# Two PSUM banks in turn for the scan's sums, a later turned copy, and column sums with standing ones

## The chip, the cores and the metric

The kernel runs on one core of one Trainium2 chip. A core has a tensor engine (PE, whose weight loads are shown apart as PEld), a vector engine (DVE), a scalar engine (ACT), GpSimd (POOL) and a sync engine (SP) that issues the DMA transfers here. Each engine works through its own queue in order and waits on semaphores for the others. On-chip memory is SBUF, and PSUM, in eight banks of 2 KiB in each of 128 partitions, takes what PE writes. The metric is the device time of one execution in microseconds (us); 13 runs are shown, and the median counts.

## The reference

The input is four images of 64x64 positions with 96 channels. Layer 0 normalises by groups, multiplies by signs of a weight, runs a 3x3 convolution on signs, and then a selective scan in four directions (by rows, by columns and both reversed) with 192 channels and 16 states each. Its core is one recurrence:

```
def step(h, inp):
    ut, dt, Bt, Ct = inp
    dA = jnp.exp(dt[..., None] * A[None])
    h = dA * h + (dt * ut)[..., None] * Bt[:, :, None, :]
    y = jnp.einsum('bkdn,bkn->bkd', h, Ct)
    return (h, y)
```

`dt` (delta) is the softplus of a small matmul of signs plus a bias. The four directions are added, normalised over channels, gated, and projected. Layer 1 is a linear attention (keys times values first) and a feed-forward layer whose numbers are rounded to small floats.

## The kernel before, in words

**The scan.** `Scans.run` (L1323) goes through 1536 pieces, each a tile of 128 partitions by 1024 positions in float32. A piece has 32 channels with 4 states each, so four pieces (q = 0..3) make a group of channels, and eight pieces fill one tile of sums. One turn of the loop, step i, issues for the pieces around i:

- `loads` and `load_sums`: DMA transfers on SP, ahead of need;
- `carry(i-1)` (L1271): ACT copies the last column of the last scan, the state that the next chunk of the same rows starts from;
- at i % 8 == 3, `evacuate(i-4)` (L1316): ACT copies the finished tile of sums `yp` to SBUF as `ys`, and SP stores it;
- `decay(i+1)` (L1231): ACT makes exp(delta·A), the tile `dA`, in PSUM. Two tiles of 128x1024 (four banks in all) are shared by all pieces, and a pool gives out whichever came free;
- `reduce(i-3)` (L1302): PE adds the products of a piece over its four states into the tile `yp` (four matmuls, each into 32 partitions), and the other directions' sums (L1307);
- `inject(i+4)`: POOL multiplies delta·u by B, the tile `w`, four pieces ahead of its scan; nine such tiles exist;
- `late_product` and `scan(i)`: DVE runs the recurrence. Either it does so in place, in dA, and DVE multiplies by C; or it writes to a tile `h` in SBUF, and POOL multiplies by C one step later. A planner (`Tally`) that adds up an estimate of both engines' work picks one, piece by piece. All DVE and POOL operations of these kinds have the line of the planner's helper, L401, and are told apart by their tiles.

**Delta, in lanes.** `prepare` (L1130) makes delta for 512 positions of 128 rows. It is a generator, and each of its parts is issued in one step, so the parts of one lane lie between the scans: eight matmuls into a tile `dps` (L1167); ACT's Abs and Relu (L1172, L1173); ACT's Exp and Ln (L1175, L1176, the latter back into the bank of `dps`); a matmul by the identity that adds the Relu (L1179); DVE's product `pd` by u; and ACT's copy of delta (L1185) with the stores. A lane starts at each i % 8 == 0, 192 in all, of which three are made before the first scan.

**Work behind.** A second generator, `back`, issues a part at each step: the prologues of the coming images (the normalisation, the convolution), and the epilogues (layer norms, attention, feed-forward). Where a lane needs u that isn't there yet, `back` is run on until it is.

The convolution in the prologue (L567 to L633) goes part by part, 8 rows of 64 at a time. A part has four steps; PE issues 5, 4, 5 and 4 of the 18 taps (L577) in them, while ACT and DVE finish the part before: signs and exp at step 1, log and exp at step 2, DVE's product `u` at step 3, and in that step also the copy of u by columns `ut`, on POOL for the first image (when no scans run) and on ACT (L614) for the others. After four parts the turned tile is stored to `utd`, from which the prologue's next stage loads it; its cast is `xr` (L659).

The group normalisation starts with sums over positions (L508 to L517): 32 matmuls (L510) that hold a 128x96 tile of x as weights and move one column of ones, all added into 96x1, copied by ACT (L514) and multiplied by a matrix that adds three channels (L516).

**PSUM.** Four of the eight banks hold the two tiles `dA`. The other four are tags of a pool with one buffer each: `b0` and `b1` for prologue and epilogue, `y` for the sums and `dps` for delta.

Of the kernel before, what the change touches and what calls it, by code (L numbers as in the profile page):

```python
# [24 lines left out]
NT = L // 128  # L25
# [28 lines left out]
def hybrid_kernel(ctx: ExitStack, tc: tile.TileContext, a: dict, out: bass.AP):  # L54
# [102 lines left out]
    def weights():  # L157
# [28 lines left out]
        def transposed(dst, srcs):  # L186

            count[0] += 1
            ps = p.ps.tile([128, 1024], BF16, name=f"tps{count[0]}", tag=("y", "dps")[count[0] % 2])
            at = 0  # L190
            for src in srcs:
                n, f = src.shape
                nc.tensor.transpose(ps[:f, at : at + n], src, identb[:n, :n])
                at += n
            nc.vector.tensor_copy(dst, ps[:f, 0:at], saturate=False if dst.dtype == F8 else None)
# [152 lines left out]
        nc.vector.tensor_copy(  # L348
            back4.rearrange("p (x d) -> p x d", x=4), ident.rearrange("p (x d) -> p x d", x=4)[:, ::-1, :]
        )  # L350
        ps = p.ps.tile([128, 512], F32, name="tpd", tag="dps")
        for g in range(3):
            for x in range(4):
                nc.tensor.matmul(
# [122 lines left out]
def prologue(c, b, xts=None):  # L477
# [11 lines left out]
    with tc.tile_pool(name=f"xg_{b}", bufs=1) as xgp:  # L489
# [3 lines left out]
        with tc.tile_pool(name=f"cv_{b}", bufs=1) as cvp:  # L493
# [6 lines left out]
            if xts is None:  # L500
# [4 lines left out]
                load_x(c, b, xts)  # L505
                yield
                yield
            csum = bank("csum", 0)[0:96, 0:1]  # L508
            for i in range(NT):
                nc.tensor.matmul(csum, xts[i // 8][:, i % 8, :], c.ones1, start=(i == 0), stop=(i == NT - 1))  # L510
                if i % 8 == 7:
                    yield
            cs = f32("cs")[0:96, 0:1]
            nc.scalar.copy(cs, csum)  # L514
            gsum = bank("gsum", 1)[0:96, 0:1]
            nc.tensor.matmul(gsum, c.grp, cs, start=True, stop=True)  # L516
            yield  # L517
            negm = f32("negm")[0:96, 0:1]
# [42 lines left out]
            parts = [(h, q) for h in range(2) for q in range(NQ8)]  # L561
            taps = [(j, t) for j in range(2) for t in range(9)]
            one = lambda h: slice(h, h + 1)
            prev = None
            two = c.p.dA.tile([128, CH], F32, name=f"cv2_{b}", tag="dA") if alone else None
            utp = sub.enter_context(tc.tile_pool(name=f"ut_{b}", bufs=1))
            for n, part in enumerate(parts + [None]):  # L567
                if part:
                    h, q = part
                    nm = f"{h}{q}"  # L570
                    at = 512 * (n % 2)
                    ps = (two[:, at : at + 512] if alone else bank("cv" + nm, 0))[0:96]
                for s in range(4):
                    if part:
                        for j, t in taps[(0, 5, 9, 14)[s] : (5, 9, 14, 18)[s]]:
                            dy, dx = divmod(t, 3)
                            nc.tensor.matmul(  # L577
                                ps, c.cw[:, j, t, 96 * h : 96 * h + 96],
                                tpad[j][:, 8 * q + dy : 8 * q + dy + 8, dx : dx + IW],
                                start=(j == 0 and t == 0), stop=(j == 1 and t == 8),  # L580
                            )
                    if prev:
                        ph, pq, pz, v, r, pn = prev
                        if s == 0:
                            c.vec.scalar_tensor_tensor(pz, pz, pv[:, ph, S_X : S_X + 1], v, ALU.mult, ALU.add)
                            c.vec.scalar_tensor_tensor(pz, r, c.oma[:, one(ph)], pz, ALU.mult, ALU.add)
                        elif s == 1:

                            sg = f32("sg" + pn)[0:96, 0:128]
                            nc.scalar.activation(  # L590
                                sg.bitcast(F8).rearrange("p (h e i) -> p h e i", h=8, e=2),
                                pz.rearrange("p (h i e) -> p h e i", h=8, e=2), AF.Sign, saturate=False,
                            )
                            for m in range(3):
                                g0 = 64 * (m // 2) + 32 * ph
                                c.later.store(xgw[g0 : g0 + 32, m % 2, 128 * pq : 128 * pq + 128], sg[m::3, :])
                            e = f32("e" + pn)[0:96]
                            nc.scalar.activation(e, pz, AF.Exp, scale=-1.0)
                        elif s == 2:
                            nc.scalar.activation(e, e, AF.Ln, bias=1.0)  # L600
                            nc.scalar.activation(e, e, AF.Exp, scale=-1.0)
                        else:
                            u = f32("u" + pn)[0:96]
                            c.vec.tensor_tensor(u, pz, e, ALU.mult)
                            c.later.store(c.ud[b][ph][:, 512 * pq : 512 * pq + 512], u)

                            if pq % 4 == 0:
                                ut = utp.tile([96, IW, 32], F32, name=f"ut{pn}_{b}", tag="ut")
                            at = 8 * (pq % 4)
                            dst, src = ut[:, :, at : at + 8], u.rearrange("p (h w) -> p w h", w=IW)  # L610
                            if alone:
                                nc.gpsimd.tensor_copy(dst, src)
                            else:
                                nc.scalar.copy(dst, src)  # L614
                            if pq % 4 == 3:
                                rows = slice(8 * pq - 24, 8 * pq + 8)
                                c.later.store(
                                    c.utd[b][ph].rearrange("p (w h) -> p w h", h=IH)[:, :, rows], ut, after=1
                                )
                    yield  # L620
                if part:
                    v, r = f32("v" + nm)[0:96], f32("r" + nm)[0:96]
                    if alone:
                        nc.vector.tensor_scalar(v, ps, c.acs[:, one(h)], c.acb[:, one(h)], ALU.mult, ALU.add)
                    else:
                        nc.scalar.activation(v, ps, AF.Identity, scale=c.acs[:, one(h)], bias=c.acb[:, one(h)])
                    nc.scalar.activation(r, ps, AF.Relu, scale=c.csc[:, one(h)], bias=c.cbias[:, one(h)])  # L627
                    pz = bank("cz" + nm, n % 2 if alone else 1)[0:96]
                    nc.tensor.matmul(
                        pz, c.winT[:, 96 * h : 96 * h + 96], xsT[:, 512 * q : 512 * q + 512], start=True, stop=True  # L630
                    )
                    prev = (h, q, pz, v, r, nm)
                    yield  # L633
            c.later.flush()
            sub.close()

# [460 lines left out]
class Scans:  # L1097
# [19 lines left out]
    def done(self, b, n):  # L1117

        return self.at > (b * NK + n) * NPC + SETTLE


    def load_signs(self, b, k):

# [6 lines left out]
    def prepare(self, spare=None):  # L1130
# [28 lines left out]
        gT = self.gs[b, k]  # L1159
        uv = self.us[:, 8 * part : 8 * part + 8] if part < 2 else self.us  # L1160
        d = spare[0] if spare else p.pd.tile([128, 2, 512], F32, name=f"pd_{nm}", tag="pd")
        ps = spare[3] if spare else p.ps.tile([128, 512], F32, name=f"dps_{nm}", tag="dps")
        pv = ps.rearrange("p (c q s) -> p s q c", q=4, s=8)
        groups = ((0, 128, 0, part),) if part < 2 else ((0, 64, 128, 0), (64, 64, 128, 1))
        wd, c0 = (c.wdz, 32 * ci + 16 * part) if part < 2 else (c.wdy, 32 * ci)
# [8 lines left out]
        yield  # L1174
        nc.scalar.activation(d[:, 0], d[:, 0], AF.Exp, scale=-1.0)  # L1175
        nc.scalar.activation(ps, d[:, 0], AF.Ln, bias=1.0)  # L1176
        yield

        nc.tensor.matmul(ps, c.ident, t, start=False, stop=True, skip_group_check=True)  # L1179
# [113 lines left out]
    def reduce(self, i):  # L1293

        c = self.c
        b, e, ci, g, q = self.pieces[i]
        if i % 8 == 0:
            self.ydone[i // 8] = c.p.ps.tile([128, 2, 256], F32, name=f"yp_{i}", tag="y")
        y, prod = self.ydone[i // 8], self.ins.pop(i)
        more = self.sums.pop(i // NQ, []) if q == NQ - 1 else []  # L1300
        for x in range(4):
            c.nc.tensor.matmul(  # L1302
                y[32 * x : 32 * x + 32, g % 2, :], c.sum4, prod[:, 256 * x : 256 * x + 256],
                start=(q == 0), stop=(q == NQ - 1 and not more), tile_position=(0, 32 * x),
            )
        for n, (src, w) in enumerate(more):
            c.nc.tensor.matmul(y[:, g % 2, :], w, src, start=False, stop=(n == len(more) - 1))  # L1307
# [15 lines left out]
    def run(self, back):  # L1323
        c, lanes, n = self.c, [], len(self.pieces)

        w = [c.p.w.tile([128, CH], F32, name=f"w_s{x}", tag="w") for x in range(7)]
        ps = [c.p.dA.tile([128, CH], F32, name=f"dA_s{x}", tag="dA") for x in range(2)]
        for x in range(3):
            half = slice(512 * (x % 2), 512 * (x % 2) + 512)
# [13 lines left out]
        self.load_dl(0)  # L1343
        for m in (1, 2):
            self.load_dl(m)
        self.decay(0)
        for i in range(AHEAD):
            self.inject(i)
        for i in range(n):
# [5 lines left out]
                self.load_sums(i)  # L1355
            if i >= 1:
                self.carry(i - 1)
            if i % 8 == 3 and i > 8:
                self.evacuate(i - 4)
            if i + 1 < n:  # L1360
                self.decay(i + 1)
            if i >= 3:
                self.reduce(i - 3)
            if i + AHEAD < n:
# [1 line left out]
            self.late_product()  # L1366
            self.scan(i)
            c.later.tick()
            if i % 8 == 0 and self.todo:
                while (self.todo[0][0], self.todo[0][1] % 2) not in c.ready:  # L1370
                    next(back)
                lanes.append(self.prepare())
# [86 lines left out]
```

## Time and profile before

| what | before |
|---|---|
| median of 13 runs | 5541.58 us (5531.6 to 5546.53) |
| profiled execution, its own time | 5546.06 us |
| its span on the profile | 5544.3 us |
| DVE busy | 5052.2 us, 91% |
| POOL busy | 4993.9 us, 90% |
| ACT busy | 3558.4 us, 64% |
| PE busy | 3434.9 us, 62% |
| granted clock of PE, mean | 0.713 |

The scans fill the span from about 260 us to 5340 us; ahead of them lie the first image's prologue and the first deltas, behind them the last image's epilogue. A scan takes 2.28 to 2.34 us, a product on DVE 1.23 us, a product on POOL 2.35 us, and a decay 1.12 us.

In a table of groups a row reads: line, engine, operation, tile written <- tiles read, shapes, count, then busy time, the mean in ns of one, and the idle time just before them with what ended it. In a table of waits a row reads: engine, tile and line that waited, <- what it waited for, then us in total, times, and the longest. In a timeline a row reads: start in us, duration in us, engine, line and operation, and in brackets the engine's idle time ahead with its releaser.

### The profile page before, as it was taken

The page shows a single profiled execution, that of the slowest core. Times are in us where ns is not written, and L with a number is a line of the kernel's source. Part 1 is how long each engine was busy: PE and PEld are TensorE (multiplying, and loading weights), DVE is VectorE, ACT ScalarE, POOL GpSimd, SP SyncE. Part 2 cuts the span into 40 slices and gives each one's busy share as a digit, 9 for nine tenths or more (in the row PEclk, how much of TensorE's full clock was granted, in tenths as well). Part 3 has the DMA queues.
Part 4 walks back from the last instruction along what each step waited for, and adds up shares of the span by engine and source line. Part 5 has one row for each costly group of instructions (what it writes and reads, how often), then busy time and mean ns, then how long its engine had stood idle before and what let it go on. Part 6 is the DMA issues. An engine that isn't in the chain of part 4 may idle for free. (4 is left out here: it accounts for less than half of the span.)

```text
span 5544.3 us, 62371 instructions
## 1 busy us (share of the span) xinstructions
PE 3434.9 (62%) x20197; PEld 1357.4 (24%) x20197; DVE 5052.2 (91%) x3237; ACT 3558.4 (64%) x5564; POOL 4993.9 (90%) x2262
## 2 busy tenths in 40 slices
PE   6456655567557766567656775544676564444677
PEld 3222222222223222222222222211232121111223
DVE  3299999999999999899999999999999999999984
ACT  4467776777666667677766667755566675655554
POOL 2199999999999999899999999999999999999980
PEclk8667776678677866677777777666787776566777
DMA  4455666766666566667666566665666566665642
GB/s 79 124 180 192 208 195 196 251 204 201 205 211 195 192 206 202 221 209 218 204 192 207 187 196 204 222 203 194 214 214 188 182 199 202 218 204 190 208 147 58
DMA packets 613244, 1069.93 MB, mean 193 GB/s; under 512 B 225083, under 2 KB 343924, under 8 KB 611124
## 3 DMA queue, kind: packets, MB, share of 16 engines
q1 hardware_dynamic: 599428, 1065.88, 61.0%
q8 instruction: 159, 2.61, 0.2%
q10 hardware_dynamic: 13488, 0.07, 0.1%
q14 instruction: 169, 1.38, 0.1%
HBM read 833.20 MB, written 229.38 MB: 192 GB/s over the span
## 5 line engine op out<-in xcount | busy, mean ns | idle before, releaser
L401 POOL TENSOR_TENSOR w<-dl,bc 128x1024 f32<-128x1024 f32 x1536 | 3580.0, 2357 | 166.6 <-PE yp L1302 94.2
L1231 ACT ACTIVATE dA<-dl,anm 128x1024 f32<-128x1024 f32 x1536 | 1715.6, 1117 | 474.4 <-DVE w L401 290.0
L1302 PE MATMUL yp<-w,sum 128*32 128x256 f32 x12288 | 1260.5, 507 | 1088.0 <-ACT ys L1316 623.8
L401 DVE TENSOR_TENSOR_SCAN dA<-dA,cy,w 128x1024 f32<-128x1024 f32 x706 | 1654.7, 2344 | 95.2 <-ACT dA L1231 84.0
L401 POOL TENSOR_TENSOR w<-h,bc 128x1024 f32<-128x1024 f32 x596 | 1402.9, 2354 | 96.0 <-DVE h L401 82.8
L401 DVE TENSOR_TENSOR w<-dA,bc 128x1024 f32<-128x1024 f32 x940 | 1151.4, 1225 | 47.7 <-DVE dA L401 0.5
L401 DVE TENSOR_TENSOR_SCAN h<-dA,cy,w 128x1024 f32<-128x1024 f32 x446 | 1043.4, 2340 | 8.2 <-ACT dA L1231 7.7
L1302 PEld LDWEIGHTS yp<-w,sum 128*32 128x32 f32 x12288 | 308.5, 127 | 2144.1 <-issue 705.5
L401 DVE TENSOR_TENSOR_SCAN dA<-dA,w 128x1024 f32<-128x1024 f32 x234 | 534.2, 2283 | 23.3 <-ACT dA L1231 20.5
L1271 ACT COPY cy<-dA 128x1 f32<-128x1 f32 x707 | 110.8, 157 | 690.7 <-DVE w L401 689.4
L577 PE MATMUL cv<-tp,cw 96*96 96x512 fp8e5 x1152 | 357.7, 454 | 82.1 <-ACT r L627 69.9
L401 DVE TENSOR_TENSOR_SCAN h<-dA,w 128x1024 f32<-128x1024 f32 x150 | 341.7, 2279 | 23.6 <-POOL w L401 23.3
L1179 PE MATMUL dps<-sp,ident 128*128 128x512 f32 x378 | 354.8, 1037 | 0.0
L1307 PE MATMUL yp<-ya,back 128*128 128x256 f32 x576 | 232.1, 523 | 0.0
L577 PEld LDWEIGHTS <-cw 96*96 96x96 fp8e5 x1152 | 157.6, 145 | 272.3 <-issue 217.2
L1271 ACT COPY cy<-h 128x1 f32<-128x1 f32 x445 | 82.6, 186 | 146.6 <-DVE h L401 145.5
L847 PE MATMUL yc<-eys,mean 96*96 96x512 f32 x240 | 136.7, 723 | 33.6 <-DVE vks L401 15.6
L1172 ACT ACTIVATE pd<-dps,dbias,pvd 128x512 f32<-128x512 f32 x189 | 144.0, 762 | 16.1 <-PE dps L1167 10.4
L1307 PEld LDWEIGHTS yp<-ya,back 128*128 128x128 f32 x576 | 120.6, 242 | 125.0 <-issue 90.4
L1173 ACT ACTIVATE sp<-dps,dbias,pvd 128x512 f32<-128x512 f32 x189 | 144.8, 766 | 0.0
L401 DVE TENSOR_TENSOR pd<-dps,pu 128x512 f32<-128x512 f32 x189 | 127.7, 675 | 5.0 <-PE dps L1179 5.0
L1316 ACT COPY ys<-yp 128x512 f32<-128x512 f32 x192 | 111.8, 582 | 30.3 <-PE yp L1307 23.3
(282 smaller groups left out, 4034.9 us busy)
## 6 DMA issues: line engine op xcount, KB each, us to landing
dl<-dld SPq DMA_DIRECT2D x768, 512.0 KB
bc<-bcd SPq DMA_DIRECT2D x512, 512.0 KB
dld<-pd SPq DMA_DIRECT2D x126, 512.0 KB
yd<-ys SPq DMA_DIRECT2D x768, 64.0 KB
dld<-pd SPq DMA_DIRECT2D x126, 256.0 KB
ya<-yd SPq DMA_DIRECT2D x192, 128.0 KB
pu<-ud SPq DMA_DIRECT2D x32, 512.0 KB
pu<-utd SPq DMA_DIRECT2D x31, 512.0 KB
```

The lines of the kernel that those rows point to most:

```text
L401: return getattr(self.eng, name)(out, *args, **kw)
L577: nc.tensor.matmul(ps, c.cw[:, j, t, 96 * h : 96 * h + 96], tpad[j][:, 8 * q + dy : 8 * q + dy + 8, dx : dx + IW], start=(j == 0 and t == ...
L847: self.c.nc.tensor.matmul(ps, w, x, start=(i == 0), stop=(i == len(pairs) - 1))
L1172: nc.scalar.activation(d[:, 0], ps, AF.Abs, scale=sc, bias=bi)
L1173: nc.scalar.activation(t, ps, AF.Relu, scale=sc, bias=bi)
L1179: nc.tensor.matmul(ps, c.ident, t, start=False, stop=True, skip_group_check=True)
L1231: c.nc.scalar.activation(t, self.dlt[i // NQ][0], AF.Exp, scale=c.anm[:, g, NQ * KORD[e] + q : NQ * KORD[e] + q + 1])
L1271: self.c.nc.scalar.copy(self.carries[g, q], h[:, CH - 1 : CH])
L1302: c.nc.tensor.matmul(y[32 * x : 32 * x + 32, g % 2, :], c.sum4, prod[:, 256 * x : 256 * x + 256], start=(q == 0), stop=(q == NQ - 1 and no ...
L1307: c.nc.tensor.matmul(y[:, g % 2, :], w, src, start=False, stop=(n == len(more) - 1))
L1316: c.nc.scalar.copy(t, y[:, :, ::-1] if k >= 2 else y)
```

## The change

Seven things are changed together.

1. The tags `y` and `dps` become `y0` and `y1`. The tile of sums of eight pieces goes to bank `y{i // 8 % 2}`, so two follow each other in different banks. Delta's tile goes to the other bank than the one in which the sums of the present piece i − 3 lie.
2. A lane starts at i % 8 == 3 rather than 0.
3. `prepare` has one more empty part, ahead of the identity matmul. With 2, its product falls to steps 0 and its copy to step 1 of the next eight.
4. In a step, `decay(i+1)` is issued ahead of `evacuate(i-4)`.
5. A fourth lane is made whole just before the first decay, with its own tiles.
6. The copy of u by columns on ACT is issued one step later, at step 0 of the following part; the taps go 5, 5, 5 and 3.
7. The column sums hold the 128x1 ones as weights and move 384 columns of x (four tiles of 96), in eight matmuls; ACT copies the row of 384, four small matmuls turn and add it into 96x1, and one more part of the generator follows.

The diff, cut to its core (the same rename of the tags in two places of the first stage, and the signs' moved lines, are left out):

```
-            csum = bank("csum", 0)[0:96, 0:1]
-            for i in range(NT):
-                nc.tensor.matmul(csum, xts[i // 8][:, i % 8, :], c.ones1, start=(i == 0), stop=(i == NT - 1))
-                if i % 8 == 7:
+            csum = bank("csum", 0)[0:1, 0 : 4 * DM]
+            for i in range(0, NT, 4):
+                nc.tensor.matmul(
+                    csum, c.ones1, xts[i // 8][:, i % 8 : i % 8 + 4, :].rearrange("p i e -> p (i e)"),
+                    start=(i == 0), stop=(i == NT - 4),
+                )
+                if i % 8 == 4:
                     yield
+            row = f32("csr")[0:1, 0 : 4 * DM]
+            nc.scalar.copy(row, csum)
+            ps = bank("cst", 1)[0:96, 0:1]
+            for i in range(4):
+                nc.tensor.matmul(
+                    ps, row[:, DM * i : DM * i + DM], c.ones1[0:1, :], start=(i == 0), stop=(i == 3)
+                )
+            yield
             cs = f32("cs")[0:96, 0:1]
-            nc.scalar.copy(cs, csum)
-            gsum = bank("gsum", 1)[0:96, 0:1]
+            nc.scalar.copy(cs, ps)
+            gsum = bank("gsum", 0)[0:96, 0:1]
...
+            def by_columns(h, q, u):
+                if q % 4 == 0:
+                    uts[h] = utp.tile([96, IW, 32], F32, name=f"ut{h}{q}_{b}", tag="ut")
+                ut, at = uts[h], 8 * (q % 4)
+                dst, src = ut[:, :, at : at + 8], u.rearrange("p (h w) -> p w h", w=IW)
+                (nc.gpsimd.tensor_copy if alone else nc.scalar.copy)(dst, src)
+                if q % 4 == 3:
+                    rows = slice(8 * q - 24, 8 * q + 8)
+                    c.later.store(c.utd[b][h].rearrange("p (w h) -> p w h", h=IH)[:, :, rows], ut, after=1)
...
-                        for j, t in taps[(0, 5, 9, 14)[s] : (5, 9, 14, 18)[s]]:
+                        for j, t in taps[5 * s : min(18, 5 * s + 5)]:
...
+                    if s == 0 and turned:
+                        by_columns(*turned)
+                        turned = None
...
+                            turned = (ph, pq, u)
                             if alone:
-                                nc.gpsimd.tensor_copy(dst, src)
-                            else:
-                                nc.scalar.copy(dst, src)
+                                by_columns(*turned)
+                                turned = None
...
+            if turned:
+                by_columns(*turned)
             c.later.flush()
...
+    def bank(self):
+        return max(0, self.at - 3) // 8 % 2
...
-        ps = spare[3] if spare else p.ps.tile([128, 512], F32, name=f"dps_{nm}", tag="dps")
+        ps = spare[3] if spare else p.ps.tile([128, 512], F32, name=f"dps_{nm}", tag=f"y{1 - self.bank()}")
...
         nc.scalar.activation(ps, d[:, 0], AF.Ln, bias=1.0)
+        yield
         yield
         nc.tensor.matmul(ps, c.ident, t, start=False, stop=True, skip_group_check=True)
...
-            self.ydone[i // 8] = c.p.ps.tile([128, 2, 256], F32, name=f"yp_{i}", tag="y")
+            self.ydone[i // 8] = c.p.ps.tile([128, 2, 256], F32, name=f"yp_{i}", tag=f"y{i // 8 % 2}")
...
-        w = [c.p.w.tile([128, CH], F32, name=f"w_s{x}", tag="w") for x in range(7)]
+        w = [c.p.w.tile([128, CH], F32, name=f"w_s{x}", tag="w") for x in range(8)]
...
+        u = c.p.pu.tile([128, CH], F32, name="pu_s", tag="pu")
+        for _ in self.prepare((w[7].rearrange("p (t l) -> p t l", t=2), w[4][:, 512:CH], u, ps[1][:, 512:CH])):
+            pass
         self.decay(0)
...
+            if i + 1 < n:
+                self.decay(i + 1)
             if i % 8 == 3 and i > 8:
                 self.evacuate(i - 4)
-            if i + 1 < n:
-                self.decay(i + 1)
...
-            if i % 8 == 0 and self.todo:
+            if i % 8 == 3 and self.todo:
```

More of the change, by code (lines that the diff above doesn't have):

```diff
@@ L188, in transposed @@
             count[0] += 1
-            ps = p.ps.tile([128, 1024], BF16, name=f"tps{count[0]}", tag=("y", "dps")[count[0] % 2])
+            ps = p.ps.tile([128, 1024], BF16, name=f"tps{count[0]}", tag=f"y{count[0] % 2}")
             at = 0
@@ L350, in weights @@
         )
-        ps = p.ps.tile([128, 512], F32, name="tpd", tag="dps")
+        ps = p.ps.tile([128, 512], F32, name="tpd", tag="y0")
         for g in range(3):
@@ L563, in prologue, with sign @@
             one = lambda h: slice(h, h + 1)
-            prev = None
+            prev = turned = None
             two = c.p.dA.tile([128, CH], F32, name=f"cv2_{b}", tag="dA") if alone else None
             utp = sub.enter_context(tc.tile_pool(name=f"ut_{b}", bufs=1))
+            uts = {}
+            def by_columns(h, q, u):
[7 more added lines that the diff above has]
+                    c.later.store(c.utd[b][h].rearrange("p (w h) -> p w h", h=IH)[:, :, rows], ut, after=1)
+            def sign(h, q, pz):
+                sg = f32(f"sg{h}{q}")[0:96, 0:128]
+                nc.scalar.activation(
+                    sg.bitcast(F8).rearrange("p (h e i) -> p h e i", h=8, e=2),
+                    pz.rearrange("p (h i e) -> p h e i", h=8, e=2), AF.Sign, saturate=False,
+                )
+                for m in range(3):
+                    g0 = 64 * (m // 2) + 32 * h
+                    c.later.store(xgw[g0 : g0 + 32, m % 2, 128 * q : 128 * q + 128], sg[m::3, :])
             for n, part in enumerate(parts + [None]):
@@ L587, in prologue @@
                         elif s == 1:
[L589 to L596, printed above, removed]
+                            sign(ph, pq, pz)
                             e = f32("e" + pn)[0:96]
@@ L601, in prologue @@
                             nc.scalar.activation(e, e, AF.Exp, scale=-1.0)
-                        else:
+                        elif s == 3:
                             u = f32("u" + pn)[0:96]
@@ L605, in prologue @@
                             c.later.store(c.ud[b][ph][:, 512 * pq : 512 * pq + 512], u)
[L607 to L610, printed above, removed]
+                            turned = (ph, pq, u)
                             if alone:
-                                nc.gpsimd.tensor_copy(dst, src)
-                            else:
-                                nc.scalar.copy(dst, src)
[L615 to L619, printed above, removed]
+                                by_columns(*turned)
+                                turned = None
                     yield
```

## The prediction

> **What bounds the kernel now.** I read the page's first part, then the busy time by stretches of time, then each engine's waits between 300 and 5330 us, and last the timeline where DVE waits.
>
> ```profile
> PE 3434.9 (62%) x20197; PEld 1357.4 (24%) x20197; DVE 5052.2 (91%) x3237; ACT 3558.4 (64%) x5564; POOL 4993.9 (90%) x2262
> ...
> 300.00:700.00 400.00, 258.98 (x1618) 100.20 (x1618) 388.41 (x242) 294.36 (x462) 395.64 (x174) 0.71 0.64 200
> 700.00:1500.00 800.00, 487.78 (x3264) 203.45 (x3262) 763.05 (x469) 568.23 (x885) 765.12 (x334) 0.71 0.68 211
> 1500.00:2500.00 1000.00, 663.89 (x3796) 253.56 (x3794) 953.49 (x584) 686.19 (x1073) 955.35 (x418) 0.71 0.64 203
> ```
>
> The columns of the stretches are PE, PEld, DVE, ACT, POOL, granted clock, DMA share, GB/s. DVE and POOL are both some 96% busy, so the busy share can't tell which sets the pace; the waits can.
>
> ```profile
> DVE dA L401 <- ACT dA L1231: 104.6, 88, 5.3
> DVE g L401 <- PE sy L847: 14.7, 6, 5.0
> DVE dA L401 <- ACT cy L1271: 7.7, 11, 1.3
> DVE h L401 <- ACT dA L1231: 6.8, 7, 3.4
> ...
> DVE dA L401 <- POOL w L401: 3.0, 4, 1.3
> ...
> POOL w L401 <- PE yp L1302: 85.6, 54, 6.8
> POOL w L401 <- DVE h L401: 72.3, 96, 2.0
> ...
> PE yp L1302 <- ACT ys L1316: 620.6, 141, 11.2
> ```
>
> DVE waits 3.0 us for POOL and 111.4 us (104.6 + 6.8) for ACT's decays. So DVE, with the decays that feed it, sets the pace. POOL's 85.6 us for PE is slack: its input is made four pieces ahead and DVE hardly misses it. PE's 620.6 us for the evacuation, the wait that the two banks remove, is one stage further off still. Between 300 and 5300 us DVE is busy 4799.5 of 5000 us (the sum of its column), so all its idle time there is 200 us, and no change that leaves its instructions alone can gain more.
>
> Where the 111.4 us come from is seen in the timeline.
>
> ```profile
> 318.17 2.28 DVE L401 TENSOR_TENSOR_SCAN h<-dA,w 128x1024 f32<-128x1024 f32 x1
> ...
> 320.49 1.12 ACT L1231 ACTIVATE dA<-dl,anm 128x1024 f32<-128x1024 f32 x1 [2.04 <-DVE h L401]
> ...
> 321.70 2.30 DVE L401 TENSOR_TENSOR_SCAN dA<-dA,w 128x1024 f32<-128x1024 f32 x1 [1.25 <-ACT dA L1231]
> ```
>
> The decay at 320.49 was given the PSUM buffer that the scan at 318.17 was just then reading, not the one that had come free a step earlier. ACT could start only when that scan ended, and DVE stood idle for the decay: 1.25 us = 1.12 + 0.13. I call this a swap of the two dA buffers. The buffers are given out by a pool in the order of release, so swaps can be read from the two programs' instruction order and waits. Before has 73, of which 50 have nothing of DVE's between the two scans; in the other 23 a product, such as pd's 0.675 us, fills part of the gap. In the trace the 50 idle 72.5 us together (some idle longer) and all 73 idle 83.5.
>
> The other stalls behind ACT sum to 39.6 us. By step of eight they are 10.7 (step 0), 14.2 (step 4) and under 5.3 in each other. Step 4's look like this:
>
> ```profile
> 845.86 0.77 ACT L686 ACTIVATE sgn<-acc,sbR 128x512 fp8e5<-128x512 f32 x1
> 846.53 0.58 ACT L1316 COPY ys<-yp 128x512 f32<-128x512 f32 x1
> 846.99 2.17 ACT L1231 ACTIVATE dA<-dl,anm 128x1024 f32<-128x1024 f32 x2
> ...
> 848.23 2.36 DVE L401 TENSOR_TENSOR_SCAN dA<-dA,cy,w 128x1024 f32<-128x1024 f32 x1 [0.67 <-ACT dA L1231]
> ```
>
> The evacuation stands ahead of the decay that the next scan needs.
>
> **The change part by part.** DVE's and POOL's instructions keep their number and kinds: 940 products on DVE and 596 on POOL in both programs.
>
> *Two banks for y.* PE's 620.6 us and POOL's 85.6 us are relieved. The sum of a piece now waits for the evacuation of eight pieces before, long over. Cover: four pieces of lead on POOL. Gain for DVE: 0, at most the 3.0 us that it waits for POOL. New wait: delta's eight matmuls (L1167) go into the bank just evacuated, and so wait for the evacuation at step 3, with the reduction, the conv and the layer sums behind them in PE's queue. The evacuation is 0.582 us on ACT, about 1.9 us after the product that its sums wait for. I take 0, since ACT reads the delta a step later; were all 187 to hold the following work by that 0.58 and a tenth of it to reach DVE, it would be +11.
> A page of the Trainium skill, "Perfetto Trace Analysis", section "Matmuls", says that independent matmul groups should rotate through PSUM banks so that the evacuation of one overlaps the next. The 620.6 us agree that the single bank stalls PE; by that rule alone the kernel would gain up to the 200 us that DVE idles, where the wait table leaves 3.0. Another page, "TensorE: Matmul & The Clock Gate", section "A second HAM failure mode: psum-queue depth-cycling", speaks against the change: cycling through banks can idle PE briefly and make its clock swing. Here the granted clock is 0.713 already, and by that page DVE's 14.7 and 22.6 us behind PE's sums (below) could grow, and were they doubled the sum would be +48.
>
> *Decay ahead of evacuation, delta's copy a step later.* At step 4 the decay no longer waits 0.582 us. Before, 192 decays had it ahead; most were covered. Of the 14.2 us at step 4 I take 12 as gone: **−12** (ends: −14.2 and −5). Delta's copy (0.578 us) and its stores land at step 1 rather than at step 5, six steps after the start rather than five; SP issues as many as before, and its next reader is pieces away. The same change of steps decides the dA buffers anew: 89 swaps, 62 unfilled. So 12 more at 1.25 = 15.0, and four more partly filled (5.1 in all: 1.25 − 0.68 is 0.57, less what fills wholly) about 1.5: **+16.5**. Ends: −5 if fewer of them are exposed than before, +25 if each of the 16 costs more because ACT's backlog meets it (of the 50, some do: 72.5 against 62.5).
>
> *Turned copy of u one step later* (L614, 1.099 us, 48 of them). ACT's 91.5 us of waiting for DVE's u go, but the decay behind was seldom late: −1 (0 to −3). The last copy of each prologue comes one step later, so its store and load come later too, and ACT waits for them in order ahead of a decay:
>
> ```profile
> 773.57 0.59 ACT L659 CAST xr<-xa 128x512 bf16<-128x512 f32 x1 [5.33 <-DMA utd<-ut]
> ...
> 774.15 1.12 ACT L1231 ACTIVATE dA<-dl,anm 128x1024 f32<-128x1024 f32 x1
> ...
> 775.37 2.36 DVE L401 TENSOR_TENSOR_SCAN dA<-dA,cy,w 128x1024 f32<-128x1024 f32 x1 [2.11 <-ACT dA L1231]
> ```
>
> Three prologues beside the scans, each up to one step of 3.5 us less the lane's own slack; I take 1.2 each: **+3.6** (0 to +8).
>
> *Column sums.* Thirty-two matmuls with 96x128 weights and one moving column become eight with one weight column and 384 moving. The old ones took 10.35 us at the start, at full clock (a record 297 ns, two for a matmul). For the new, the nearest row is the 512-column one into 96 rows (L847 fc, 1.080 us a record, two records): 8 × 2 × 1.08 × 384/512 = 13.0 at its clock, half of that at full clock. Beside the scans ACT waited 13.9 us for these sums and DVE 6.4 of them. Now the copy of 384 sums, four tiny matmuls and one more step follow. Three times: **+1.5** (−3 to +6). At the start, where it is the path but PE then waits for POOL's slab copies: **+2** (−2 to +4).
>
> *Delta prepared for a fourth piece before the first decay.* Before, from 262.05 to 275.85 us POOL makes six inputs back to back, and the scan at 278.21 waits 9.21 us for POOL. The new copy, product (0.675) and the wait for its load lie beside that, if the load lands by about 270, where the bytes of that queue end: **0** (−1 to +12, the first decay being at 260.24 and the load up to that much later). One product less in the loop: −0.7, set against one alignment.
>
> Steps of the background work shift by one per prologue, so matmul waits such as g <- sy (14.7 us) and sq <- yc (22.6 us of DVE's time) fall elsewhere: 0 (±8).
>
> Sum: −12 + 16.5 − 1 + 3.6 + 1.5 + 2 = **+10.6 us** against this execution's 5546.06. That is 4.5 above the median of the runs, so 5541.6 + 10.6 = 5552.
>
> **The rivals.**
> (a) *Faster: ACT's queue is evened out by more than step 4.* Between two decays ACT has over 4.0 us of work 125 times before and 74 after (order, with the row's durations), the excess over 4.0 us falling from 39.5 to 12.1 us. For it: DVE's 39.6 us of other stalls. Against: half of these wait for PE's four-matmul sums or a DMA, not for ACT's own work. If all 27.4 us went rather than 12, the sum is −5; with swaps at half, −13; with the 5.0 us that pd waits for PE gone too, −18: 5523. It decides where swaps cost under 6.
> (b) *Equal: swaps and the evacuation's gain cancel.* If the 12 more swaps fall where a wait existed anyway: 5536 to 5546.
> (c) *Slower by more: delta's matmuls block PE behind the evacuation* (+11), or the fourth load lands late (+12): 5563 to 5575. For it: sq <- yc shows that DVE does lose when PE is late, 22.6 us over 12 times. Against: PE idles over a third of the time.
> (d) *The change does not do what it says:* PE's wait moves whole from L1302 to L1167, because y and delta share each bank in turn. Then PE stays blocked about 600 us, POOL's 85.6 stay too, and the time is that of the swaps and the evacuation, 5546.
>
> **How the numbers follow.** 0.2% (11 us) is about what a measurement of this kernel can tell from no change. My own sum has chance 0.5, spread ±10 around +10.6, thus 0.24 slower, 0.23 within, 0.03 faster; (a) 0.2 (0.17 faster, 0.03 within); (b) and (d) 0.1 (0.06 within, 0.02 each side); (c) 0.2 (0.18 slower, 0.02 within). Together faster 0.22, within 0.34, slower 0.44. The range reaches down to (a)'s −14 and up to (c): 5527 to 5577; the likeliest's own range is 5542 to 5562.
>
> **What would show it.** PE's wait for ys gone or under 60 us; POOL's for PE down by about 32 us (what its waits at steps 1 and 2 sum to), without a gain of DVE's; DVE idles of exactly 1.25 us up from 50 to about 62; stalls at step 4 down from 14.2 to 2; DVE's wait behind xr up; and DVE's idle time between 300 and 5300 us near 210 rather than 200. Wrong if DVE's wait for ACT falls below 95 us, or if delta's L1167 shows a wait for ys of hundreds of us together with new DVE waits for pd.

## The result, and the profile after

The changed kernel takes 5553.49 us (median of 10 runs, 5545.77 to 5557.95), against 5539.03 us (44 runs) of the kernel before: a ratio of 1.0026, 95% interval 1.0018 to 1.0034. It is 14.4 us slower, with 5552 forecast. The profiled execution of after took 5557.95 us, with a span of 5556.2, 11.9 us more than that of before: 3.4 us had been lost when scan 16 (counted from 0) began, 11.4 were lost from there to the end of the last scan, and 2.9 were won back behind it. The last scan ends at 5418.7 us before and 5433.4 after, not near 5340 as said ahead, so the windows up to 5330 us leave out the last 90 to 100 us of scans.

The busy times and the stretches of after hardly differ from before:

```profile
PE 3454.8 (62%) x20037; PEld 1359.9 (24%) x20037; DVE 5050.8 (91%) x3237; ACT 3568.7 (64%) x5568; POOL 4993.6 (90%) x2262
...
300.00:700.00 400.00, 259.10 (x1587) 96.42 (x1586) 387.73 (x241) 294.12 (x461) 393.75 (x173) 0.71 0.62 198
700.00:1500.00 800.00, 501.74 (x3216) 205.53 (x3215) 760.50 (x469) 569.34 (x883) 763.13 (x333) 0.69 0.67 211
1500.00:2500.00 1000.00, 642.11 (x3741) 243.54 (x3741) 951.86 (x581) 684.20 (x1069) 955.25 (x419) 0.73 0.63 203
```

Between 300 and 5300 us DVE is busy 4792.2 us rather than 4799.5: the same instructions, with 207.8 us of idle time among them instead of 200.5 (forecast near 210). The waits tell where it went. Waits of after, first DVE's, then POOL's, then PE's, between 300 and 5330 us:

```profile
DVE dA L401 <- ACT dA L1259: 101.3, 85, 4.5
DVE h L401 <- ACT dA L1259: 19.2, 7, 6.1
DVE g L401 <- PE sy L870: 10.3, 6, 4.9
DVE dA L401 <- ACT cy L1299: 8.5, 10, 1.3
...
POOL w L401 <- DVE h L401: 99.3, 113, 3.5
POOL w L401 <- PE yp L1330: 51.0, 40, 3.7
...
PE dps L1194 <- ACT ys L1344: 616.7, 153, 7.8
PE yp L1330 <- POOL w L401: 302.6, 144, 5.9
```

Three things are to be seen. DVE waits 120.5 us for ACT's decays instead of 111.4. POOL waits 34.6 us less for PE, and DVE gains nothing by it: its own waits for POOL's `w` are 6.6 us instead of 3.0. And PE's wait for the evacuation did not go: 620.6 us stood at the sums' matmuls, 616.7 us stand now at delta's (L1194), which go into the bank that is being evacuated.

The swap of the two dA buffers looks as it did before, only there are more of them:

```profile
341.18 2.28 DVE L401 TENSOR_TENSOR_SCAN h<-dA,w 128x1024 f32<-128x1024 f32 x1
...
343.49 1.12 ACT L1259 ACTIVATE dA<-dl,anm 128x1024 f32<-128x1024 f32 x1 [1.46 <-DVE h L401]
...
344.71 2.30 DVE L401 TENSOR_TENSOR_SCAN dA<-dA,w 128x1024 f32<-128x1024 f32 x1 [1.25 <-ACT dA L1259]
```

I put each idle time of DVE behind ACT either to a swap (the decay of that piece waits, in the program, for the scan just before) or to another cause, over the whole of both traces:

| DVE idle behind ACT, us | before | after |
|---|---|---|
| swaps without an instruction between the scans | 72.5 (50) | 82.0 (62) |
| swaps with one between | 11.0 (23) | 14.4 (27) |
| all swaps | 83.5 | 96.4 |
| everything else | 39.6 | 38.5 |
| of this at step 4 of eight | 14.2 | 5.3 |
| of this at step 6 | 2.5 | 13.7 |

So by this count the rest of ACT's stalls changed in its places but not in its sum, and the swaps' 12.9 us are most of the 14.4. The count is a wide one: it gives a swap all the idle time at its piece, also where ACT came to the decay later still because of other work (in one case of before 4.0 us later, behind the column sums). A strict count takes only the idle time of scans that waited for a decay which itself had waited for the end of the scan just before. It gives 53.6 us (48 times) before and 73.1 us (64 times) after, 19.5 more.

### The profile page after: what moved, and what is told of

Read it like the earlier page. It is cut to its first block, busy times and chain, and to the rows that moved or that the text cites. A ratio compares the mean times of both kernels' runs of the same rounds, so it can differ in the third digit from the quotient of the medians.

```text
span 5556.2 us, 62039 instructions
## 1 busy us (share of the span) xinstructions
PE 3454.8 (62%) x20037; PEld 1359.9 (24%) x20037; DVE 5050.8 (91%) x3237; ACT 3568.7 (64%) x5568; POOL 4993.6 (90%) x2262
## 5 line engine op out<-in xcount | busy, mean ns | idle before, releaser
L1330 PE MATMUL yp<-w,sum 128*32 128x256 f32 x12288 | 1300.7, 518 | 490.2 <-POOL w L401 325.2
L1194 PE MATMUL dps<-gT,wdz 128*128 128x64 fp8e5 x1000 | 119.6, 324 | 453.7 <-ACT ys L1344 423.3
L1207 PE MATMUL dps<-sp,ident 128*128 128x512 f32 x376 | 274.5, 820 | 65.3 <-ACT dps L1203 65.3
L1194 PEld LDWEIGHTS <-wdz 128*128 128x128 fp8e5 x1024 | 100.0, 157 | 538.8 <-issue 502.0
L1194 PE MATMUL dps<-gT,wdy 128*128 128x64 fp8e5 x504 | 56.9, 311 | 193.4 <-ACT ys L1344 193.4
L870 PE MATMUL yc<-eys,mean 96*96 96x512 f32 x240 | 139.3, 735 | 29.8 <-DVE vks L401 11.4
```

What stands on the lines that cost most here:

```text
L870: self.c.nc.tensor.matmul(ps, w, x, start=(i == 0), stop=(i == len(pairs) - 1))
L1194: nc.tensor.matmul(pv[:, s], wd[:, k, s], gT[:, :, c0 : c0 + 16], start=(s == 0), stop=(s == 7))
L1330: c.nc.tensor.matmul(y[32 * x : 32 * x + 32, g % 2, :], c.sum4, prod[:, 256 * x : 256 * x + 256], start=(q == 0), stop=(q == NQ - 1 and no ...
```

## The experiments

All times are medians in us; a ratio is to runs of the kernel before on the same chip. Four groups of kernels ran apart, and the medians of before beside them were 5536.24 (both kernels with fixed buffers, and the two edits of after without them), 5534.52 (the order in before, the lanes with fixed buffers, the early signs, the column sums), 5537.9 (the turned copy, the order in after) and 5536.59 (what is left with the two banks). Where DVE's idle time is given by cause, it is put to what ACT itself waited for longest just before the decay.

### Fixed buffers for dA, in both kernels

The edit gives even pieces one tag and odd pieces another, so that a decay can only take the buffer of two pieces ago:

```diff
-        f=pool("fp", 8), bc=pool("bcp", 5), dl=pool("dlp", 3), dA=pool("dAp", 2, space=PSUM),
+        f=pool("fp", 8), bc=pool("bcp", 5), dl=pool("dlp", 3), dA=pool("dAp", 1, space=PSUM),
...
-        t = c.p.dA.tile([128, CH], F32, name=f"dA_{i}", tag="dA")
+        t = c.p.dA.tile([128, CH], F32, name=f"dA_{i}", tag=f"dA{i % 2}")
```

(The other tiles of that pool, at the start and the end, get `dA0` or `dA1` likewise.) On the kernel before:

> Before, with the dA tile of an even piece always in one buffer and that of an odd piece always in the other, so that a decay never waits for the scan just before it. Theory (swaps of the two dA buffers): the 73 swaps and their 57 to 84 us of DVE idle go, and the time falls from 5539 to 5460-5485 us; no DVE idle of 1.25 us behind a decay is left. Rival (the idle time only moves on, to POOL or PE, each of which is as busy or blocked): under 20 us gained, 5520-5540, with DVE's waits for POOL's w up by tens of us.

Measured: 5483.9, ratio 0.9906 (0.9893 to 0.9918), 52 us less. On the kernel after:

> After, with the same fixed dA buffers. Theory: its 89 swaps and 74 to 84 us go, 5465-5480 us, and the gap between the two kernels (+14) disappears or turns: after with fixed buffers is 0 to 10 us faster than before with fixed buffers, since its evacuation no longer stands ahead of a decay. Rival (the 14 us come from delta's matmuls waiting for the evacuation, from the start, and from the shifted background steps): the gap stays at +10 to +20.

Measured: 5479.95, ratio 0.9899 (0.9886 to 0.9912). DVE's waits of before with fixed buffers, then of after with fixed buffers:

```profile
DVE dA L401 <- ACT dA L1231: 56.3, 48, 5.7
DVE g L401 <- PE sy L847: 17.0, 7, 5.6
DVE h L401 <- ACT dA L1231: 9.6, 7, 4.5
```

```profile
DVE dA L401 <- ACT dA L1259: 40.7, 33, 4.4
DVE h L401 <- ACT dA L1259: 25.8, 10, 4.4
DVE g L401 <- PE sy L870: 11.4, 8, 4.4
```

What a step without the swap looks like is seen in the timeline of after with fixed buffers. The decay at 318.94 starts 0.31 us after the start of the scan at 318.63 rather than at its end, and no idle time stands at the scan of 321.41:

```profile
318.63 2.28 DVE L401 TENSOR_TENSOR_SCAN h<-dA,w 128x1024 f32<-128x1024 f32 x1
...
318.94 1.12 ACT L1259 ACTIVATE dA<-dl,anm 128x1024 f32<-128x1024 f32 x1
...
320.83 0.67 DVE L401 TENSOR_TENSOR pd<-dps,pu 128x512 f32<-128x512 f32 x1
...
321.41 2.29 DVE L401 TENSOR_TENSOR_SCAN dA<-dA,w 128x1024 f32<-128x1024 f32 x1
```

The swaps cause the idle time: with the buffers fixed it is gone in both kernels (the strict count gives 0), and nothing else was touched. The gap between the two kernels goes from 1.0026 − 1 to 0.9899 − 0.9906, that is from +14 to −4 us, the latter within its interval; the move of 18 us is known to some 11 us, from the three intervals together. So the swaps that the change adds make its slowdown.

By the ratios, before gained 52 us and after 70 (73.5 in the medians, which were taken apart). That is less than the wide count had put to the swaps (83.5 and 96.4 us), and about what the strict count had (53.6 and 73.1). The rest of the stalls behind ACT seems to rise, from 39.6 to 66.6 us and from 38.5 to 67.3. Most of that is the counting: ACT's other late work at the swapped pieces now stands under its own name. With the strict count the rest had been 69.5 us in before and 61.8 in after already, so it is not shown that the idle time moved on to other late work.

### Evacuation ahead of the decay again

```diff
-            if i + 1 < n:
-                self.decay(i + 1)
             if i % 8 == 3 and i > 8:
                 self.evacuate(i - 4)
+            if i + 1 < n:
+                self.decay(i + 1)
```

In the kernel after:

> After, with the evacuation ahead of the decay again. Theory: swaps fall from 89 to 80 (unfilled from 62 to 57: -6 us) and the stalls of the step after the evacuation come back (+9 to +12): +3 to +6, 5556-5560 us. Rival (the order of the two is what costs, through the swaps it makes): faster by over 5 us.

Measured: 5542.36, ratio 1.0011 (1.0003 to 1.002): 11 us less than after in the medians and 8 by the ratios, whose intervals overlap. The theory, which had it slower, missed. Its swaps idle 85.5 us instead of 96.4 (66.8 instead of 73.1 by the strict count), which is of that size, and the other stalls behind ACT stay at 38.9. The stall that should have come back at step 4 came back by 2.0 us only (5.3 to 7.3).

With fixed buffers in both, so that no swap is mixed in:

> After with fixed dA buffers (5480 us) and the evacuation ahead of the decay. Theory (with the lanes at step 3, ACT has no delta work beside the evacuation, so the order is worth nothing by itself, and the 11 us that undoing it saved in the changed kernel were swaps): within 4 us of 5480; PE's 552 us behind ys fall by over 100. Rival (the later evacuation itself costs, through PE): 6 or more faster.

Measured: 5490.46, ratio 0.9908 (0.9895 to 0.9922), against 0.9899 with the decay first: 10 us slower in the medians, 5 by the ratios, with overlapping intervals. So the rival is out, and whether the order is worth nothing, as the theory had it, or some 5 us stays open. In the traces step 4 is 11.1 us worse (7.9 to 19.0), steps 5 and 6 are 8.3 us better together, and DVE's idle time from the 16th scan to the last differs by 3.2 us. PE's wait for ys falls from 552.0 to 350.5 us and buys nothing. The other way round, the order alone in the kernel before with fixed buffers:

> Before with fixed dA buffers (5484 us) and the decay ahead of the evacuation; no swaps in either, so the order is priced alone. Theory (the order alone takes the stall of step 4 away): DVE's idle behind ACT at step 4 falls from 21.6 to under 10 us and the time by about 12, to 5468-5476. Rival (it is the later start of the lanes that keeps ACT's delta work out of that step): step 4 keeps over 15 us, and the time is within 4 us of 5484.

Measured: 5489.57, ratio 0.9918 (0.9903 to 0.9933). Step 4 does fall, from 21.6 to 10.2 us, but the time does not: it is 6 us above that of before with fixed buffers, with overlapping intervals, where 12 below had been expected. With only one bank for y the evacuation that now waits behind a decay holds PE longer, and PE holds others. Waits of DVE, PE and POOL in before with fixed buffers and the decay first:

```profile
DVE pd L401 <- PE dps L1179: 12.7, 14, 4.4
...
PE yp L1302 <- ACT ys L1316: 779.8, 155, 12.7
...
POOL w L401 <- PE yp L1302: 84.3, 56, 7.2
```

Without the new order these were 3.9, 598.0 and 64.4 us. So the order takes its 11 us from step 4 in both kernels, and no gain of time from it is clear of the noise. With one bank the time gets rather longer, beside more waiting in PE's queue; with two, 8.3 of the 11.1 us are lost again at the two steps after.

### Lanes one step after the evacuation

```diff
-            if i % 8 == 3 and self.todo:
+            if i % 8 == 4 and self.todo:
...
         nc.scalar.activation(ps, d[:, 0], AF.Ln, bias=1.0)
         yield
-        yield
```

In the kernel after:

> After, with the lanes starting a step later (i % 8 == 4) and without the empty part, so that delta's matmuls come a step after the evacuation and the end of a lane stays where it is. Theory: PE's 617 us of waiting for ys go, which alone is worth only the 9 to 11 us that DVE lost behind late delta matmuls; the swaps fall from 89 to 69 (unfilled 62 to 48: -17.5); together -25 to -30, 5524-5530 us. Rival (PE's blocked time sets the pace): over 50 us faster. Second rival (neither matters): 5548-5560.

Measured: 5533.16, ratio 0.9991 (0.9982 to 1.0). It is 20 us faster than after, a little less than expected. The swaps idle 72.8 us instead of 96.4 (60.5 instead of 73.1 by the strict count), and DVE's idle time behind late delta matmuls falls from 12.4 to 0.7 us; each is of the size of a part of the gain, and how they share it is open. PE's wait of 616.7 us for ys did not go but becomes 192.0, and 284.9 instead of 65.3 stand at the identity matmul behind ACT's log:

```profile
PE yp L1329 <- POOL w L401: 311.3, 168, 6.7
PE dps L1206 <- ACT dps L1203: 284.9, 108, 7.8
PE dps L1194 <- ACT ys L1343: 192.0, 98, 6.4
```

With fixed buffers, where the swaps can't differ:

> After with fixed dA buffers (5480 us) and the lanes at i % 8 == 4 without the empty part. Theory (PE's wait for ys is slack, and only the wait of three lanes for their first load of signs is shortened by a step): PE's 552 us behind ys fall below 250, DVE's idle behind late delta from 11.6 to 0-6, the time to 5470-5478. Rival (PE's blocked time reaches DVE in many small pieces): 5455 or less.

Measured: 5477.93, ratio 0.9894 (0.9877 to 0.991), against 0.9899. PE's wait for ys falls by 386 us, from 552.0 to 165.8, but 201 of them come back at the identity matmul, where 55.8 us had stood:

```profile
PE dps L1206 <- ACT dps L1203: 256.7, 102, 6.8
PE dps L1194 <- ACT ys L1343: 165.8, 79, 5.4
```

PE's idle time as a whole, between 300 and 5330 us, falls from 1837.7 to 1775.3. These 62 us are worth 2 us in the medians, well within the intervals; 5455 or less, the rival, is out.

### The first signs of an image loaded earlier

Behind the stalls of step 6 in after are three lanes, the first of images 2 to 4. Each loads the signs that delta is made from and needs them at once. In the trace of after, PE waits for the load, ACT for PE, and the decay stands behind ACT's first delta step:

```profile
4056.95 1.01 PE L1194 MATMUL dps<-gT,wdz 128*128 128x64 fp8e5 x8 [8.69 <-DMA gT<-gTd]
...
4058.00 0.78 ACT L1199 ACTIVATE pd<-dps,dbias,pvd 128x512 f32<-128x512 f32 x1 [7.83 <-PE dps L1194]
4058.68 0.77 ACT L1200 ACTIVATE sp<-dps,dbias,pvd 128x512 f32<-128x512 f32 x1
...
4059.53 1.12 ACT L1259 ACTIVATE dA<-dl,anm 128x1024 f32<-128x1024 f32 x1
...
4060.75 2.35 DVE L401 TENSOR_TENSOR_SCAN h<-dA,cy,w 128x1024 f32<-128x1024 f32 x1 [6.10 <-ACT dA L1259]
```

PE waits about 30 us for these loads in both kernels (30.1 and 30.4, three times). DVE paid 1.5 us for it before and 12.4 after. The edit, on top of fixed buffers and lanes at step 4:

```diff
             self.load_signs(b, KORD[KORD.index(k) + 1])
+        if (ci, k) == (NCH - 1, KORD[-1]) and (b + 1, KORD[0]) not in self.gs and (b + 1, KORD[0] % 2) in c.ready:
+            self.load_signs(b + 1, KORD[0])
```

> As the one before, and the first signs of images 2 to 4 are loaded some 20 steps earlier instead of in the lane that needs them. Theory: PE's three waits of 8 to 12 us for them go, with what is left of DVE's idle behind them: 0 to 8 us under the kernel with lanes at 4, 5465-5475. Rival (the transfer waits for the prologue's own stores, and SP is held with it): no gain, or slower by up to 5.

Measured: 5468.01, ratio 0.9878 (0.9863 to 0.9892). PE's wait for the load is gone from the table. Against the kernel without the edit (5477.93) the intervals overlap, so the gain of 10 us is not certain by itself. Nor can much of it come from DVE's waits for delta, which had already fallen to 1.4 us with the lanes at step 4; what else gave way is open. The kernel as a whole is 67 us faster than before and beats both.

### The column sums, the turned copy, and what is left with the two banks

Each on the kernel after with fixed buffers (5479.95, ratio 0.9899). The old column sums:

```diff
-            for i in range(0, NT, 4):
+            for i in range(NT):
                 nc.tensor.matmul(
-                    csum, c.ones1, xts[i // 8][:, i % 8 : i % 8 + 4, :].rearrange("p i e -> p (i e)"),
-                    start=(i == 0), stop=(i == NT - 4),
+                    csum, xts[i // 8][:, i % 8, :], c.ones1, start=(i == 0), stop=(i == NT - 1),
                 )
...
```

> After with fixed dA buffers (5480 us) and the old column sums. Theory (the new sums gain a little beside the scans, where DVE lost 6.4 to 6.8 us behind the old ones, and nothing at the start): +3 to +8, 5483-5488. Rival (as forecast: the longer chain costs 3.5): 5473-5478.

Measured: 5488.56, ratio 0.9915 (0.9901 to 0.993): 8.6 us slower in the medians, with overlapping intervals, and not faster, as the rival had it. The turned copy in the step of u again:

```diff
-                        for j, t in taps[5 * s : min(18, 5 * s + 5)]:
+                        for j, t in taps[(0, 5, 9, 14)[s] : (5, 9, 14, 18)[s]]:
...
-                            if alone:
-                                by_columns(*turned)
-                                turned = None
+                            by_columns(*turned)
+                            turned = None
```

> After with fixed dA buffers (5480 us) and the turned copy on ACT in the step of u again (taps 5, 4, 5, 4). Theory (as forecast: the later copy holds the load of the turned u, and with it ACT's xr, by 2 to 4 us in all, and saves 1 of waiting for u): 2 to 5 us faster, 5475-5478, DVE's idle behind xr from 7.9 to 5-6. Rival (ACT's waiting for u, 91 us in the kernel before, costs more than the trace shows): 5 or more slower.

Measured: 5480.35, ratio 0.9886 (0.987 to 0.9901): no difference in the median, but 7 us faster by the ratios, whose intervals overlap. DVE's idle behind xr is 4.5 us instead of 7.9, as expected; what that is worth is within the noise. All three undone, so that the banks, the later lanes and the fourth lane at the start remain:

> After with fixed dA buffers, and the column sums, the turned copy and the order of evacuation and decay as before: what is left of the change is the two banks, the later lanes and the fourth lane at the start. Theory (the banks give DVE nothing; the later lanes make the first signs of three images later, some 5 to 10 us): 5484-5496, not faster than before with fixed buffers (5484). Rival (the two banks free PE and POOL and are worth their 600 us in part): under 5475.

Measured: 5484.78, ratio 0.9909 (0.9895 to 0.9922), the same as before with fixed buffers (5483.9, 0.9906). The two banks, the later lanes and the fourth lane together are worth nothing here. The banks were not run without the later lanes: DVE's idle time behind late delta matmuls is 14.4 us in this trace against 6.6 in that of before with fixed buffers, so a gain of some us from the banks could be hidden behind the lanes. One of the size of PE's wait could not. The Trainium skill, "Perfetto Trace Analysis", section "Matmuls", would have matmul groups rotate through banks; the 620.6 us agreed that PE was blocked, and in these runs relieving it won no time that can be measured.

## Why the prediction was right, step by step

**What bounds the kernel**: right. Freeing DVE of its swaps gave 52 and some 70 us; freeing PE of 386 us of its wait for ys, and of 62 us of idle time, gave 2, within the intervals.

**Swaps, +16.5**: right in kind and about in size. The trace of after has them at 12.9 us more idle by the wide count and 19.5 by the strict one, with 62 of them unfilled as read from the instruction order. With the buffers fixed in both kernels the gap moves by 18 us (from +14 to −4). The end of +25, for swaps that cost more each, did not come: the 62 idle 82.0 us, 1.32 each, the 50 idled 72.5, 1.45 each. The four more with a product between were put at 1.5 and idle 3.4 more; the working's "5.1 in all" for such swaps stands against 11.0 us in the trace of before (83.5 − 72.5).

**Decay ahead of evacuation, −12**: mis-sized. Step 4 lost 8.9 us of its stall, to 5.3 rather than 2, and the sum of the other stalls behind ACT stayed (39.6 and 38.5), mostly because step 6 got 11.2 us more (below). The term was read as time won. With fixed buffers the order by itself moved the time by 6 us to the slower in before, and undoing it in after made it 5 us slower by the ratios, neither clear of the noise.

**New wait at delta's matmuls, taken as 0**: right that they now wait for ys, and for nothing on DVE's side: pd waited 5.0 us for PE before and 2.4 after. I had still written that PE's wait for ys would be gone or under 60 us. That was wrong, and rival (d) had it: the wait moved whole, 616.7 of 620.6 us. No cost of it is seen at DVE. POOL's wait for PE fell by 34.6 us, forecast as 32, without a gain; that it would stay, as (d) had it, was wrong.

**First lanes of an image**, a term that is missing: 12.4 us of DVE's idle time behind late delta in after against 1.5 before, 10.9 us that the sum left out. With the lanes at step 4 it was 0.7. Rival (c) had delta's matmuls late, and blamed the evacuation; the releaser in the trace is the load of the signs.

**Column sums, +3.5**: the sign was probably wrong beside the scans. At the start the eight matmuls took 7.96 us rather than 10.35 (the working gave 6.5 at full clock and 13.0 at half), but the copy and the small matmuls behind them took that back: from the first matmul of the sums to the end of ACT's `negm` it was 12.5 us before and 13.0 after, so 0.5 where 2 was forecast. That the old 10.35 us were at full clock is not shown either. The first record of a granted clock lies at 55.5 us in before and at 36.5 us in after, and the clock column reads 1.00 ahead of it; yet the records of the new sums come every 640 ns up to 36.3 us and every 322 ns from 36.7 us on. Beside the scans DVE's 6.4 us behind the old sums are not in the trace of after. Undoing them cost 8.6 us in the medians, with overlapping intervals. Which part of the longer chain saved it was not tried.

**Turned copy, −1 + 3.6**: DVE's idle behind xr rose from 6.1 to 8.3 us, so +2.2 with nothing seen of the −1. Undone by itself it moved nothing that is clear of the noise.

**The start**: the fourth lane cost nothing, as forecast: the third scan began 4.0 us later, at 282.23 us instead of 278.21, but POOL's first input had also begun 4.0 us later (266.06 instead of 262.05). Of these 4 us, 3.6 are there at the end of the first image's convolution, and came about within it (below), not at the sums.

So the total was right by more than its parts were, and that it came within 2 us is luck: the change was 14.4 us against 10.6, and the base, 5539.03, was 2.5 us under the one forecast from. The swaps decided the sign, as forecast; but the gain at step 4 was taken back by the late signs, which the sum did not have, and the errors on the sums and at the start were of either sign.

## What to carry to other kernels

Before asking what a stall of a blocked engine is worth, ask who waits for that engine: PE's 620 us held up nothing that could be measured, while 1.25 us on the engine that sets the pace, some dozens of times, decided the result. Where two buffers of a pool are taken in turn by pieces that are released in varying order, fix the turn with two tags: any reordering of unrelated work can otherwise deal out the buffers anew and cost or win more than the edit itself. And before pricing a wait, count only the idle time that this wait itself ended last: all the idle time at the swapped pieces was 83 and 96 us, the part that ended with the swap 54 and 73, and 52 and some 70 were won.

## What the runs showed of the hardware

The start of this kernel depends on how the granted clock falls on it. The convolution of the first image takes 18 matmuls for each part. A matmul that lies in a stretch with a granted clock of 1.00 has a record of 381 ns in the mean, and in one with 0.50 of 632 ns; the traces' records of the clock hold only these two values. The 18 matmuls take 4.08 us where the clock is 1.00 throughout, 5.75 where its mean is 0.70, and 7.4 where it is 0.54; from part to part, with the work between, mostly 5.8 or 7.5 us. Of the 14 intervals from the end of the second part to that of the last, 4 to 6 are slow in the thirteen traces, and scan 16 (counted from 0) starts between 316.5 us and 328.2 us. Before had 4 (321.7), after 6 (325.1). After was 0.9 us ahead at the first matmul of this convolution (82.9 us against 83.8) and 3.6 us behind at the end of its last (190.0 against 186.4). So the 3.4 us that after is late at scan 16 arose in this stretch, where its parts met the low clock more often. Whether the change has to do with that, one trace each can't settle.

With two banks for y the mean granted clock was 0.699 to 0.708 in the profiles of ten kernels, and with one bank 0.713 to 0.721 in three. The ten also have the later lanes, so it is not shown that the banks lower the clock. The Trainium skill, "TensorE: Matmul & The Clock Gate", section "A second HAM failure mode: psum-queue depth-cycling", describes a clock that swings where banks are cycled. The lower clock agrees, but no time went with it: with fixed buffers the kernels with two banks and with one, both with the old sums, copy and order, differ by 0.9 us.
